# Batch 2's pair scatters, batch 3's in one expert slot, a declared wait, and a layer norm's two GpSimd steps: four small edits in an attention and expert kernel

## The chip, the cores and the metric

The kernel runs on one core of one Trainium2 chip. The metric is the device time of one execution in microseconds (us). A core has several engines that run side by side, each with its own queue of instructions in fixed order: TensorE (PE, matrix products), VectorE (DVE), ScalarE (ACT), GpSimd (POOL) and SyncE (SP, which here only issues DMAs). An instruction waits on semaphores for results of other engines.

## What is computed

The reference is one transformer block over x of 4 batches, 1024 positions and 256 channels, in float32:

```python
q_lat, k_lat, v_lat = ...                        # x @ W*_down: 16 heads with 64 latents each
q, k, v = ...                                    # 16 per head; half of q's and k's get a rotary embedding
scores = jnp.einsum('bhqd,bhkd->bhqk', q, k) * scale
scores = jnp.where(causal[None, None], scores, -jnp.inf)
y = jnp.einsum('bhqk,bhkd->bhqd', softmax(scores), v)
x = _layernorm(x + y @ Wc)
gates = _sinkhorn((x @ router_w.T + router_b) / temp)   # 3 iterations, over experts and over positions
topk_vals, topk_idx = jax.lax.top_k(gates, 2)
all_out = (relu(x @ wg[e]) * (x @ wp[e])) @ wo[e]       # 8 experts
x = _layernorm(x + sum over the two chosen experts of gate * all_out)
```

Only the two chosen experts count for a position, so the kernel computes only those.

## The kernel before

**Attention.** The batches are worked on one after the other, in units of a batch, a group of heads and a range of queries (`attend`, called from the main loop). The scores are computed twice: first for the maximum of each row (matmul L351, reductions L372 and L381 on DVE), then again, transposed, for the exponentials (matmul L456, ACT L467) and the products with the values (L436). While batch b is attended to, side work is fed in between by hand-written planners. A `Lane` is a list of generators; `give(budget)` lets it put instructions until the costs that the generators yield have used up the budget. `lane` carries projections and `finish`, `side` carries the routing, `places` the scatters. The order on each engine is then set by a scheduler that simulates a timeline from this program order, the priorities and the dependencies.

**The end of a batch's attention.** `finish` (L577 on) normalises the attention's output (L599 transposes, L604 and L606 on DVE), multiplies it with Wc (L615, L625), adds x (L628), and calls `layernorm` (L545 on): statistics on DVE (L549, L550), then two steps on POOL, the addition of epsilon to the variance (L552) and the power of minus one half (L553), then the scaling on DVE (L555). Its rows go to DRAM (`x_rows`, stores at L653 and L657).

**Routing and pairs.** `route` computes scores, Sinkhorn's iterations and the two best experts of each position, counts how many positions each expert has so far, and so gives each (position, choice) a row `ati` (tile `so_i`, L838) in a list in DRAM, `pairs`, that is ordered by expert. `scatter` (L842) writes an entry (the position's row, the row of the result, the gate) into that list: per batch 16 indirect DMAs of 128 entries each, issued on POOL (L848). After each it yields a cost: SCAT = 3.5 for batches 0 and 1, SCAT3 = 2.5 for batch 2, 1.0 for batch 3. For batches 0 to 2 `places.give(1.0)` comes at each step of the attention. Two marks order each scatter: `in_turn`, and `after(ins, latest[0])`, a dependency on the latest ACT instruction that the planner has put, so that it is not issued too early. `apart("pairs", ...)` (L561) declares that it has no dependency on any earlier scatter of pairs, since each touches rows of its own.

**The experts.** A `Slot` is 512 rows of one expert from the list: `first[0..7]` the first 512 of each (list 0, expert 0 to 7), `second[0..7]` the next 512 (list 1, expert 7 to 0), then further slots of 256 rows. `pairs_of` loads list entries (SP, L946), `gather` (L952) fetches the rows of x by indirect DMA on POOL (L957, four for 512 rows), `rows` transposes them (L1002) and splits them in a high and a low part, `slot` (L1005) computes: per quarter of the hidden width gate and linear products in three passes (`mm3`, L195 to L197), relu (ACT L1019), product (DVE L1020), split; then per 128 rows the output product, ACT's scaling by the gate (`eo`, L1038), and an indirect DMA that adds the rows to `results` in DRAM (POOL L1039). The adds of a slot wait for those of the slot before.

Batches 0 to 2 fill list 0 early enough for the first slots; batch 3 is attended to last, and its pairs come while the experts run: `slot` calls `places.give(1.0)` after each of its four quarters and each of its four blocks of 128 rows, in the slots `first[5]` and `first[6]`, so 16 times in all. What is left is put behind slot 6 (`places.until`). The load of list 1 for `second[0]` must wait for all of batch 3's pairs. A gather for a slot of list 0 beyond the third has a mark for the scheduler (not a semaphore) that it comes after `spread[0]`, the POOL step of the latest layer norm that is stored there: L552's addition.

Of the kernel before, what the change touches and what calls it, by code (L numbers as in the profile page):

```python
# [14 lines left out]
ALU = mybir.AluOpType  # L15
# [4 lines left out]
SIDE3 = 0.2  # L20
YB = 2
XG = 2
SCAT, SCAT3 = 3.5, 2.5
DZ = 3
HB = 6
SURE = 3
# [8 lines left out]
EPS_LN = 1e-5  # L35
# [6 lines left out]
def kernel(  # L42
# [16 lines left out]
    nc = tc.nc  # L59
    B, T, C = x_in.shape  # L60
# [3 lines left out]
    E, _, FF = wg_in.shape  # L64
# [38 lines left out]
    def mx_tile(name):  # L103
        return ps_mx.tile([P, QC], F32, tag="mx", name=name)
# [4 lines left out]
    def st_tile(name):  # L109
        return ps_st.tile([P, QC], F32, tag="st", name=name)  # L110
# [59 lines left out]
    neg_half = const.tile([P, BPQ], F32, name="neg_half")  # L170
# [15 lines left out]
    def split(hi, lo, src, sub=None):  # L186

        nc.scalar.copy(hi, src)  # L188
        (sub or nc.vector).tensor_tensor(lo, src, hi.bitcast(F32), ALU.subtract)  # L189

    def mm3(ps, terms):

        n = len(terms)
        for i, (sh, sl, mh, ml) in enumerate(terms):
            nc.tensor.matmul(ps, lhsT=sh, rhs=mh, start=(i == 0), stop=False)  # L195
            nc.tensor.matmul(ps, lhsT=sh, rhs=ml, start=False, stop=False)  # L196
            nc.tensor.matmul(ps, lhsT=sl, rhs=mh, start=False, stop=(i == n - 1))  # L197
# [210 lines left out]
    def in_turn(ins):  # L408

        if diagonal[0] is not None:  # L410
            tc.add_manual_dep(
                ins.ins, diagonal[0].ins.name,
                mybir.DependencyInfo(mybir.DependencyClass.NoSync, mybir.DependencyReason.SCHED_ONLY),
                reason="the attention goes first",
            )
# [127 lines left out]
    spread = [None]  # L543

    def layernorm(x, n):  # L545
        mv = small.tile([P, BPQ, 2], F32, tag="mv", name=f"mv_{n}", bufs=2)
        for i in range(BPQ):
            st = small.tile([P, 6], F32, tag="bnst", name=f"bnst_{n}_{i}")
            nc.vector.bn_stats(st, x[:, i, :])  # L549
            nc.vector.bn_aggr(mv[:, i, :], st)  # L550
        rstd = small.tile([P, BPQ], F32, tag="rstd", name=f"rstd_{n}", bufs=2)
        spread[0] = nc.gpsimd.tensor_scalar_add(rstd, mv[:, :, 1], EPS_LN)  # L552
        nc.gpsimd.tensor_tensor(rstd, rstd, neg_half, ALU.pow)  # L553
        for i in range(BPQ):
            nc.vector.tensor_scalar(  # L555
                x[:, i, :], x[:, i, :], mv[:, i, 0:1], rstd[:, i : i + 1], ALU.subtract, ALU.mult
            )
# [3 lines left out]
    def apart(what, kind, ins, others):  # L561

        seen = no_deps.setdefault(what, {})
        for o in others:
            for i in seen.get(o, ()):
                tc.declare_no_dep(ins.ins, i, reason="they touch rows of their own")
        seen.setdefault(kind, []).append(ins.ins)
# [9 lines left out]
    def finish(b, halves=range(NQC), alone=False):  # L577
# [3 lines left out]
        for half in halves:  # L581
# [58 lines left out]
            for i0 in range(0, BPQ, wide):  # L640
# [6 lines left out]
                for i in range(i0, i0 + wide):  # L647
                    f_out(i)
                    yield 0.9
            layernorm(x1, n)  # L650
            r0 = b * T + half * QC
            store = nc.sync if alone else nc.gpsimd
# [32 lines left out]
    def route(b):  # L685
# [152 lines left out]
        nc.vector.tensor_copy(ati, at)  # L838
        yield 0.0
        places.add(f"S{b}", scatter(b, ent, ati))  # L840

    def scatter(b, ent, ati):  # L842

        for n in range(NB):
            for k in range(2):
                while not hole[0]:
                    yield WAIT
                ins = nc.gpsimd.indirect_dma_start(  # L848
                    out=pairs[:, :],
                    out_offset=bass.IndirectOffsetOnAxis(ap=ati[:, k, n : n + 1], axis=0),  # L850
                    in_=ent[:, n, k, :], in_offset=None,
                )
                in_turn(ins)
                after(ins, latest[0])
                apart("pairs", "last" if b == B - 1 else "write", ins, ("last", "write", "early"))
                yield SCAT if b < B - 2 else SCAT3 if b < B - 1 else 1.0


    def tab(name, shape):
# [56 lines left out]
    def after(ins, other):  # L916
        tc.add_manual_dep(
            ins.ins, other.ins.name,
            mybir.DependencyInfo(mybir.DependencyClass.Sync, mybir.DependencyReason.DATA),
            reason="rows that both may touch",  # L920
        )
# [83 lines left out]
    def slot(k, between):  # L1005

        R = k.rows
        hs = []
        for f in range(NFC):
            cut = slice(f * P, (f + 1) * P)  # L1010
            if 2 * R > QC:
                gate, lin = (mx_tile(f"{i}p{k.name}_{f}") for i in "gl")
            else:
                both = mx_tile(f"gp{k.name}_{f}")
                gate, lin = both[:, :R], both[:, R:]
            for (h_, l_), ps in zip(k.hl, (gate, lin)):
                mm3(ps, [(h_[:, c, cut], l_[:, c, cut], k.xh[:, c, :R], k.xl[:, c, :R]) for c in range(CC)])
            r = early.tile([P, ER], F32, tag="relu", name=f"relu{k.name}_{f}", bufs=3)[:, :R]
            latest[0] = nc.scalar.activation(r, gate, AF.Relu)  # L1019
            nc.vector.tensor_tensor(r, r, lin, ALU.mult)  # L1020
            hh, hlo = (
                ffn.tile([P, ER], F32R, tag=i, name=f"{i}{k.name}_{f}", bufs=HB)[:, :R] for i in ("hh", "hl")
            )
            split(hh, hlo, r)
            hs.append((hh, hlo))
            next(between, None)
            if k in first[E - 3 : E - 1]:
                places.give(1.0)
        mine = []
        h_, l_ = k.hl[2]  # L1030
        for j in range(k.blocks):
            cut = slice(j * P, (j + 1) * P)
            if j % 2 == 0:
                both = st_tile(f"eo{k.name}_{j}")
            po = both[:, j % 2 * C : (j % 2 + 1) * C]
            mm3(po, [(hs[f][0][:, cut], hs[f][1][:, cut], h_[:, f], l_[:, f]) for f in range(NFC)])
            eo = early.tile([P, C], F32, tag="eo", name=f"eo{k.name}_{j}", bufs=EO)
            latest[0] = nc.scalar.activation(eo, po, AF.Copy, scale=k.ent[:, j, 2:3].bitcast(F32))  # L1038
            ins = nc.gpsimd.indirect_dma_start(  # L1039
                out=results[:, :], out_offset=bass.IndirectOffsetOnAxis(ap=k.ent[:, j, 1:2], axis=0),  # L1040
                in_=eo, in_offset=None, compute_op=ALU.add,
            )
            apart(f"results{k.name}", "add", ins, ("add",))
            if not k.which:
                apart("results", "early", ins, ("last",))
            for o in added:
                after(ins, o)
            mine.append(ins)
            next(between, None)
            if k in first[E - 3 : E - 1]:  # L1050
                places.give(1.0)
        added[:] = mine
        for _ in between:
            pass
# [59 lines left out]
    first = [Slot(0, e) for e in range(E)]  # L1114
# [13 lines left out]
    for i, unit in enumerate(units):  # L1128
        b, gs, qcs = unit
# [97 lines left out]
    def run(keys, given=()):  # L1227
        drain(begin(keys, 0, given))
        for n, key in enumerate(keys):
            slot(key, begin(keys, n + 1, given))  # L1230
            if key is first[E - 2]:
                places.until(f"S{B - 1}")
# [31 lines left out]
    for i in range(n_z):  # L1264
        z = zs.pop(i)
        mv = small.tile([P, BPQ, 2], F32, tag="mv", name=f"mv_f{i}", bufs=2)
# [4 lines left out]
        rstd = small.tile([P, BPQ], F32, tag="rstdz", name=f"rstd_f{i}", bufs=4)  # L1271
# [97 lines left out]
```

## Time and profile before

| | |
|---|---|
| time, median of 3 runs | 1090.79 us (1086.51 to 1091.84) |
| profiled execution | 1095.9 us, span 1094.2 us, 18114 instructions |
| mean granted TensorE clock | 0.957 |
| busy share PE, DVE, ACT, POOL | 89%, 67%, 57%, 44% |
| DMA moved | 119.67 MB, mean 109 GB/s |
| pairs on POOL (L848) | 64, 67.8 us in all, 1060 ns mean |
| adds to results on POOL (L1039) | 64, 107.2 us, 1674 ns mean |
| gathers on POOL (L957) | 64, 65.1 us, 1017 ns mean |
| POOL idle before pairs | 75.9 us, of which 57.5 us for ACT's L467 |

The profiled execution is one run; its own time is 5.1 us above the median of the timed runs. In a row of a timeline stand the start in us, the busy time, engine, line, operation, the tiles written and read, and in brackets the idle time of the engine before it and what ended it. "issue" there is time in which nothing that the profile shows was waited for, "remote" a release whose origin the profile does not see.

### The profile page before, as it was taken

How to read it: one execution, taken by the hardware profiler on the slowest of the kernel's cores; microseconds unless marked ns; L12 is line 12 of the kernel's file. 1: busy time of each engine (PE TensorE's matmuls, PEld its weight loads, DVE VectorE, ACT ScalarE, POOL GpSimd, SP SyncE). 2: the span in 40 equal slices, each digit the busy share in tenths (PEclk: the TensorE clock that was granted, in tenths of full speed). 3: DMA queues.
4: the chain of work that ended last, by engine and by line, in shares of the span. 5: the costliest groups of instructions: out<-in, count | busy, mean ns of one | idle time of the engine just before them, and what ended most of it. 6: DMA issues, size and time to landing. Idle time of an engine off the chain costs nothing.

```text
span 1094.2 us, 18114 instructions
## 1 busy us (share of the span) xinstructions
PE 975.8 (89%) x6436; PEld 608.2 (56%) x6436; DVE 734.9 (67%) x1622; ACT 625.4 (57%) x1314; POOL 479.1 (44%) x543
## 2 busy tenths in 40 slices
PE   6689999999999999989999996899999399999970
PEld 4555433455544455543444443488888288888860
DVE  4767787888888778787757882286686145555536
ACT  3445666765665755666656663656565145555533
POOL 6177511022352632552223215427557655554535
PEclk9889999999989999999999998999999699999985
DMA  6574420231240330333143220357555345656537
GB/s 245 165 213 121 117 86 18 76 117 33 95 121 17 107 114 5 127 80 98 47 102 98 46 70 2 99 174 186 141 125 123 69 109 113 172 113 164 123 36 307
DMA packets 71363, 119.67 MB, mean 109 GB/s; under 512 B 16416, under 2 KB 43040, under 8 KB 70880
## 3 DMA queue, kind: packets, MB, share of 16 engines
q1 hardware_dynamic: 48544, 81.76, 24.3%
q0 software_dynamic: 20672, 36.41, 15.5%
q8 instruction: 53, 0.87, 0.3%
q10 hardware_dynamic: 2048, 0.27, 0.2%
q14 instruction: 46, 0.38, 0.1%
HBM read 82.52 MB, written 35.60 MB: 108 GB/s over the span
## 4 chain that ended last, share of the span: by engine, by line
PE 74%; DMA 7%; DVE 6%; ACT 5%; SPq 4%; issue 2%; POOL 2%; another core or an unknown queue 1%; ACTq 0%; POOLq 0%; DVEq 0%
PE y L436 12%; PE s L351 11%; PE sT L456 10%; SPq L336 3%; PE gp L197 3%; PE gp L196 3%; PE gp L195 3%; PE eo L197 3%; PE eo L196 3%; PE eo L195 3%; PE po L625 3%; PE lp L197 2%; PE lp L196 2%; ACT pT L467 2%; PE lp L195 2%
## 5 line engine op out<-in xcount | busy, mean ns | idle before, releaser
L467 ACT ACTIVATE pT<-sT 128x512 f32<-128x512 f32 (+1 forms) x608 | 327.1, 575 | 180.8 <-PE sT L456 129.2
L372 DVE TENSOR_REDUCE mx<-s 128x1 f32<-128x384 f32 (+3 forms) x352 | 216.6, 633 | 36.2 <-PE s L368 35.1
L351 PE MATMUL s<-ks,qs 96*128 96x512 bf16 (+3 forms) x768 | 212.4, 333 | 19.4 <-DMA ks<-parts 10.8
L456 PE MATMUL sT<-qs,ks 98*128 98x512 bf16 (+3 forms) x768 | 215.5, 330 | 9.0 <-ACT pT L467 6.9
L381 DVE TENSOR_REDUCE mx<-s 128x1 f32<-128x512 f32 x256 | 171.4, 682 | 47.6 <-PE s L351 47.1
L474 POOL TENSOR_SCALAR_AFFINE_SELECT pT<-pT 128x512 f32<-128x512 f32 x112 | 70.7, 638 | 254.9 <-ACT pT L467 250.4
L436 PE MATMUL y<-pT,va 128*32 128x512 f32 (+3 forms) x1536 | 169.2, 503 | 4.4 <-ACT pT L467 3.1
L1039 POOL DMA_INDIRECT results<-eo,ents x64 | 107.2, 1674 | 82.6 <-ACT eo L1038 65.4
L351 PEld LDWEIGHTS <-qs 96*128 96x128 bf16 x768 | 70.8, 99 | 120.3 <-issue 89.7
L456 PEld LDWEIGHTS <-ks 98*128 98x128 bf16 x768 | 69.8, 99 | 89.6 <-issue 57.4
L848 POOL DMA_INDIRECT pairs<-ent,so_i x64 | 67.8, 1060 | 75.9 <-ACT pT L467 57.5
L368 PE MATMUL s<-mask,ident_b 128*128 128x128 bf16 (+2 forms) x352 | 87.1, 248 | 0.0
L1020 DVE TENSOR_TENSOR relu<-relu,lp 128x512 f32<-128x512 f32 x64 | 43.7, 683 | 60.1 <-ACT relu L1019 30.6
L195 PE MATMUL eo<-wh,hh 128*128 128x256 f32 x280 | 80.5, 289 | 0.9 <-ACT eo L1038 0.6
L957 POOL DMA_INDIRECT xg<-x_rows,ents x64 | 65.1, 1017 | 33.6 <-issue 16.1
L196 PE MATMUL eo<-wl,hh 128*128 128x256 f32 x280 | 79.0, 284 | 0.0
L189 DVE TENSOR_TENSOR wl<-w,wh 128x512 fp32r<-128x512 f32 x108 | 69.3, 684 | 14.3 <-ACT wh L188 13.8
L197 PE MATMUL eo<-wh,hl 128*128 128x256 f32 x280 | 77.7, 284 | 0.0
L1019 ACT ACTIVATE relu<-gp 128x512 f32<-128x512 f32 (+1 forms) x76 | 42.7, 563 | 59.6 <-PE gp L197 49.9
L436 PEld LDWEIGHTS y<-pT,va 128*32 128x32 f32 x1536 | 31.8, 108 | 64.6 <-issue 46.5
L195 PE MATMUL gp<-xh,wh 128*128 128x512 f32 (+1 forms) x176 | 65.0, 376 | 2.1 <-ACT xh L188 1.2
L196 PE MATMUL gp<-xl,wh 128*128 128x512 f32 (+1 forms) x176 | 65.6, 374 | 0.0
(213 smaller groups left out, 1849.0 us busy)
## 6 DMA issues: line engine op xcount, KB each, us to landing
ks<-parts SPq DMA_DIRECT2D x90, 128.0 KB
w<-in_wg_dram SPq DMA_DIRECT2D x18, 512.0 KB
w<-in_wp_dram SPq DMA_DIRECT2D x18, 512.0 KB
w<-in_wo_dram SPq DMA_DIRECT2D x18, 512.0 KB
qs<-parts SPq DMA_DIRECT2D x66, 128.0 KB
parts<-lv POOLq DMA_DIRECT2D x12, 384.0 KB
parts<-lv POOLq DMA_DIRECT2D x24, 192.0 KB
xh<-in_x_t_dram SPq DMA_DIRECT2D x8, 512.0 KB
```

What stands on the lines that cost most here:

```text
L195: nc.tensor.matmul(ps, lhsT=sh, rhs=mh, start=(i == 0), stop=False)
L196: nc.tensor.matmul(ps, lhsT=sh, rhs=ml, start=False, stop=False)
L197: nc.tensor.matmul(ps, lhsT=sl, rhs=mh, start=False, stop=(i == n - 1))
L351: nc.tensor.matmul(ps, lhsT=q(h, half)[:NROW, t * P : (t + 1) * P], rhs=k(h, kc)[:NROW, :w], start=first, stop=last,)
L368: nc.tensor.matmul(each[:, :, w - P :], lhsT=ident_b, rhs=mask.unsqueeze(1).to_broadcast([P, m, P]), start=False, stop=True,)
L372: nc.vector.tensor_reduce(mx_of[:, half, h0 : h0 + m, t], each, AX.X, ALU.max)
L381: nc.vector.tensor_reduce(mx_of[:, kc, h, t : t + 1], ps, AX.X, ALU.max)
L436: nc.tensor.matmul(acc[g, qc][SLOT * h : SLOT * (h + 1), lo:], lhsT=va[b % 2][:, kb, at : at + SLOT], rhs=pT[:, h, lo:], start=(kb == 0), ...
L456: nc.tensor.matmul(st[:, h % m * w : (h % m + 1) * w], lhsT=k(h, kb // BPQ)[: NROW + 2, kb % BPQ * P : (kb % BPQ + 1) * P], rhs=q(h, qc)[: ...
L467: latest[0] = nc.scalar.activation(pT[:, h + 1 - m : h + 1, lo:], st[:, : m * w].rearrange("p (h t) -> p h t", t=w), AF.Exp, scale=scale,)
L474: diagonal[0] = nc.gpsimd.affine_select(out=block, in_=block, pattern=[[0, HG], [1, P]], compare_op=ALU.is_ge, fill=0.0, base=0, channel_m ...
L1039: ins = nc.gpsimd.indirect_dma_start(out=results[:, :], out_offset=bass.IndirectOffsetOnAxis(ap=k.ent[:, j, 1:2], axis=0), in_=eo, in_offs ...
```

## The change

Four edits. The cost of a pair of batch 2 becomes 2.0 instead of 2.5, so `places.give` puts them at a closer distance in the attention's steps. Each scatter declares a wait for the landing of the last but one of the same batch (`after(ins, sent[-2])`), ahead of the call of `apart`. A pair of batch 3 costs 0.5 instead of 1.0, and only slot 6 gives, so that each of its eight calls puts two pairs. And `spread[0]` names the layer norm's second POOL step (the power) instead of its first, so that gathers for the later slots come behind both.

```diff
-SCAT, SCAT3 = 3.5, 2.5
+SCAT, SCAT3 = 3.5, 2.0
...
         rstd = small.tile([P, BPQ], F32, tag="rstd", name=f"rstd_{n}", bufs=2)
-        spread[0] = nc.gpsimd.tensor_scalar_add(rstd, mv[:, :, 1], EPS_LN)
-        nc.gpsimd.tensor_tensor(rstd, rstd, neg_half, ALU.pow)
+        nc.gpsimd.tensor_scalar_add(rstd, mv[:, :, 1], EPS_LN)
+        spread[0] = nc.gpsimd.tensor_tensor(rstd, rstd, neg_half, ALU.pow)
...
     def scatter(b, ent, ati):
 
+
+        sent = []
         for n in range(NB):
             for k in range(2):
...
                 in_turn(ins)
                 after(ins, latest[0])
+                if len(sent) > 1:
+                    after(ins, sent[-2])
+                sent.append(ins)
                 apart("pairs", "last" if b == B - 1 else "write", ins, ("last", "write", "early"))
-                yield SCAT if b < B - 2 else SCAT3 if b < B - 1 else 1.0
+                yield SCAT if b < B - 2 else SCAT3 if b < B - 1 else 0.5
...
             next(between, None)
-            if k in first[E - 3 : E - 1]:
+            if k is first[E - 2]:
                 places.give(1.0)
...
             next(between, None)
-            if k in first[E - 3 : E - 1]:
+            if k is first[E - 2]:
                 places.give(1.0)
```

## The prediction

> **What bounds the kernel now.** I read the page's busy shares first (PE 975.8 us of a span of 1094.2), then the table of windows of 10 us, PE's list of waits between 640 and 900 us, and last the timelines of the engines around the places that the change touches. In the table the columns are: window, its length, PE, PEld, DVE, ACT, POOL busy with counts, PEclk, DMA share, GB/s.
>
> ```profile
> 650.00:660.00 10.00, 9.80 (x91) 5.39 (x90) 5.18 (x26) 6.61 (x15) 5.69 (x7) 1.00 0.02 3
> 660.00:670.00 10.00, 4.13 (x36) 2.06 (x33) 1.20 (x5) 1.20 (x2) 7.57 (x9) 0.83 0.03 2
> 670.00:680.00 10.00, 8.06 (x42) 4.57 (x42) 3.89 (x12) 4.96 (x10) 3.04 (x4) 0.66 0.02 2
> ...
> 840.00:850.00 10.00, 10.00 (x58) 8.78 (x57) 4.45 (x7) 3.18 (x6) 8.17 (x7) 1.00 0.71 180
> 850.00:860.00 10.00, 4.41 (x26) 3.72 (x25) 3.29 (x5) 4.14 (x8) 8.17 (x7) 0.89 0.43 69
> 860.00:870.00 10.00, 0.00 (x0) 0.00 (x0) 0.00 (x0) 0.00 (x0) 4.43 (x5) 0.50 0.35 50
> 870.00:880.00 10.00, 6.94 (x27) 4.93 (x28) 1.29 (x2) 1.55 (x3) 7.56 (x9) 0.59 0.35 106
> ```
>
> PE is full nearly everywhere, so work and order on PE set the time, but for two holes, both beside POOL's indirect DMAs: 660 to 675, where batch 2's pairs are scattered, and 854 to 871, after batch 3's. PE's waits name them.
>
> ```profile
> PE xgT_ps L1002 <- DMA xg<-x_rows,ents: 18.7, 5, 16.4
> PE yt_ps L599 <- DVE yn L606: 5.6, 1, 5.6
> PE y L436 <- ACT pT L467: 3.1, 1, 3.1
> ```
>
> The 16.4 us is the second hole, the 5.6 the first, and the 3.1 a smaller third one at 702.6, beside gathers. The changed program, built and laid beside the old one, has PE, DVE, ACT and SP in unchanged order up to the experts' stage; POOL's order first differs in batch 2's pairs. So four places are to be costed.
>
> **The new wait.** It adds nothing: `apart`, called right behind, declares no dependency between this scatter and every earlier one of its kind, the last but one among them. With the lines of `sent` deleted the built program is the same, instruction for instruction. Even a working wait would find its pair landed: the pair of 655.23 has landed by 657.3, and the next but one starts at 657.82. Behind it on POOL would stand the later pairs, the layer norm's steps, for which DVE L555 waits, and the gathers, for which PE's xgT waits. Cost 0.
>
> **Batch 2's pairs (2.5 to 2.0).** Each pair waits for an ACT instruction that the planner put ahead of it. Before, the waits let twelve go back to back, 1.27 us each, and the thirteenth waits until ACT moves again. First POOL, then DVE and ACT:
>
> ```profile
> 669.20 0.96 POOL L848 DMA_INDIRECT pairs<-ent,so_i  x1 [0.30 <-issue]
> 673.45 0.96 POOL L848 DMA_INDIRECT pairs<-ent,so_i  x1 [3.29 <-ACT pT L467]
> ```
>
> ```profile
> 669.62 0.26 DVE L604 RECIPROCAL rec<-yt_ps 128x16 f32<-128x16 f32 x1 [8.70 <-remote]
> ```
>
> ```profile
> 672.57 1.09 ACT L467 ACTIVATE pT<-sT 128x512 f32<-128x512 f32 x2 [8.77 <-PE yt_ps L599]
> ```
>
> PE had ended the matmuls for which ACT and DVE wait by 664.9, and was itself idle for 5.62 us from there. They start 5 to 8 us later, when the burst stops. The same is seen at 699.86 (ACT 5.2 us idle behind gathers) and at 886.41 (relu 3.8 us late). In the mixed run of pairs and adds from 831 to 862 there is no such delay. I read it so: some 6 us into an unbroken run of indirect DMAs, PE's releases no longer reach the others until the run stops. The mechanism is not shown; the rows are. Here a rule of the Trainium skill speaks against me: "SBUF — State Buffer", section "Who interferes with whom", says that DMA never contends with a compute engine, and PE and ACT wait for nobody; at most descriptor generation on POOL suffers. By the rule a longer burst costs PE nothing and this edit is worth 0; by the row the freeze lasts as long as the burst. I take the row.
>
> In the changed program the first seven pairs wait for no ACT instruction, the eighth to fourteenth for instructions that all ended before the freeze (the same counts let the twelfth go at 669.20), the fifteenth for none; only the sixteenth waits for a later one. Fifteen in a row: 3 x 1.27 = 3.8 us longer, and the hole on PE grows by it. Bounds: -2 if the freeze ends by itself, since DVE's release at 669.62 lies before the twelfth's end, and the last pairs no longer break up 673 to 682; +4.5 with the slower clock behind it (0.66 at 670 to 680). I take **+3.8**.
>
> Then the sixteenth goes about 677, before 681.33, the list's load and the gathers begin sooner, and the two stores of rows (L653, L657) stand behind seven gathers instead of four, so that runs of seven and five replace four and eight. The third hole (3.14 us) may shrink by 1 to 3, or move: I take **-1**, from -3 to +1.
>
> **Layer norm.** The two POOL steps with the gathers between them:
>
> ```profile
> 729.26 0.24 POOL L552 TENSOR_SCALAR rstd<-mv 128x4 f32<-128x4 f32 x1 [25.80 <-DVE mv L550]
> ...
> 735.33 1.06 POOL L553 TENSOR_TENSOR rstd<-rstd,neg_half 128x4 f32<-128x4 f32 x1
> ```
>
> Now L553 follows at once: 735.33 - 729.5 = 5.8 us sooner, and the four gathers (1.27 us each) come 1.06 later. DVE L555, the router and Sinkhorn's small steps start up to 5.8 us earlier. PE is full from 707 to 854, though, and what comes out, batch 3's positions (so_i, ready at 816.9), waits: in the changed order the pairs stand behind the experts' relu of slot 6 (826.3 + 0.6). So it gives nothing. What it can take: a Sinkhorn transpose, put some 10 us earlier in PE's order, could meet a DVE that isn't ready. **0**, from 0 to +2; without the cover of the full PE it would have been -5.8.
>
> **Batch 3's pairs in slot 6 alone.** This is the tail of POOL's run, from its timeline, and then, from the chain that ended last (start, us, what), the two transfers behind it:
>
> ```profile
> 850.51 1.60 POOL L1039 DMA_INDIRECT results<-eo,ents  x1 [0.30 <-issue]
> ...
> 860.48 1.58 POOL L1039 DMA_INDIRECT results<-eo,ents  x1 [0.30 <-issue]
> 862.36 0.98 POOL L848 DMA_INDIRECT pairs<-ent,so_i  x1 [0.30 <-issue]
> 868.00 0.99 POOL L957 DMA_INDIRECT xg<-x_rows,ents  x1 [4.66 <-DMA ents<-pairs]
> ```
>
> ```profile
> 862.36 2.16 DMA pairs<-ent,so_i
> 864.53 2.60 DMA ents<-pairs
> ```
>
> PE's work ends at 854.4; from there the end is POOL's: the last pair, its landing, the load of list 1, gathers, and PE at 870.84. POOL has no pause from 831 on, and slot 6's first add starts at 850.51, 5 us after its eo (ACT 845.06 + 0.48). The change puts pairs 1 to 8 behind slot 4's and 5's adds, and the other eight two by two behind each add of slot 6. An add is 1.58 + 0.30 = 1.88, a pair 0.97 + 0.30 = 1.27. The add eo_5_0 waits for the landing of eo_4_3 (3.04 us idle at 831.24); moved ahead of the pairs it goes at about 825.1. Then come 8 pairs and 4 adds, 10.2 + 7.5 = 17.7: POOL is at slot 6's first add by 843 to 845, and now waits for ACT until 845.8. Ahead of the last pair stand 4 adds and 7 pairs: 845.8 + 7.5 + 8.9 = 862.2; the second add waits 0.5 more (ACT 850.28 + 0.48), and two or three pairs take 1.43 to 1.49 as now (+0.7). That is 863.4, **+1.1** on 862.36; bounds -0.2 (no stretching) and +2.5. PE's slots 5 to 7 and the work on each side of the hole are unchanged.
>
> The second half from 886 on has a full PE; a weight load and two adds trade places: 0, within 1.
>
> **Sum**: 3.8 - 1 + 0 + 0 + 1.1 = +3.9 us. The profiled execution took 1095.9 (span 1094.2 and 1.7 around it); it becomes 1099.8. It lies 5.1 above the median of 1090.8; the difference carried over, 1094.7.
>
> **Rivals.**
> *The burst costs nothing in an unprofiled run* (or its freeze does not grow). For it: no mechanism is shown. Against: the profiled run is only 5.1 us above the median, and the late releases cost PE 12.8 us by its idle times (5.62 + 1.35 + 0.73 from 664.9 to 673, 3.14 + 0.55 around 700, 1.43 at 886), so most of it is there without the profiler. Then only the tail counts: about 1091.9.
> *Slower: POOL comes late to slot 6.* At 818.58 and 820.73 two pairs took 1.84 and 3.04 us instead of 0.97. If the eight pairs after eo_5_0 stretch alike (0.9 to 2.1 each), POOL passes 845.8; from there, so from about 2 us of stretching on, each microsecond lands in the hole. Four such pairs bring some 4 us more: 1098.7. For: DVE's splits run beside them. Against: the pairs from 833 to 862 took at most 1.49.
> *Faster: the early finish of batch 2's pairs counts.* If the freeze ends by itself, the third hole goes (-3.7) and the last four pairs' pauses with it (-2), against the tail's +1.1: 1086; were the burst's freeze to go altogether (-7.7), 1079. For: DVE's release at 669.62. Against: ACT's at 672.57.
>
> **Numbers.** Forecast 0.46 (1094.7, own range 1091 to 1098.5), no growth 0.20, slower 0.18, faster 0.16. What this measurement can tell from no change is about 0.5%, 5.5 us: faster is below 1085.3, slower above 1096.2. Faster takes 0.14 from its case; slower all of its own, most of it above, plus a third of the forecast: 0.33; the rest, 0.53, is same. Range 1085 to 1101.
>
> **What would show it.** Fifteen pairs without a pause from about 655, DVE L604 idle 11 to 13 us and PE's 5.6 grown to 9 or so; L553 right behind L552; the last pair 8.5 to 10 us after PE's last matmul of slot 7 and PE's 16.4 at 17 to 18. Wrong, if the hole at 660 has the same size with fifteen pairs, or if pairs are seen spaced by landings.

## The result, and the profile after

The changed kernel takes 1095.24 us (median of 18 runs, 1089.64 to 1099.44), the kernel before 1089.36 in 18 runs beside it. The ratio is 1.0051, with a 95% interval from 1.0035 to 1.0067: 5.6 us slower, 3.8 to 7.3. The forecast was +3.9 us.

PE's waits between 640 and 900 us, as before: the hole before list 1 has grown from 16.4 to 18.4, and the wait at the pairs has come apart into three, of 3.51, 2.05 and 5.17 us: 10.7 together, where it had been 5.62, 1.35 and 0.73, or 7.7.

```profile
PE xgT_ps L1007 <- DMA xg<-x_rows,ents: 20.1, 4, 18.4
PE sT L456 <- ACT pT L467: 7.9, 3, 5.2
PE yt_ps L599 <- DVE rec L604: 3.5, 1, 3.5
PE ynT_ps L615 <- DVE x L628: 2.1, 1, 2.1
```

In the windows of 10 us, PE's busy time (the first number behind the length) falls to 2.34 from 660 to 670, where it was 4.13, and ACT does nothing at all there. The first pair went 3.4 us earlier in this profile than in the one before (651.82 against 655.23), so the same window does not hold quite the same work.

```profile
660.00:670.00 10.00, 2.34 (x14) 1.22 (x15) 1.71 (x5) 0.00 (x0) 7.57 (x9) 0.66 0.03 2
670.00:680.00 10.00, 6.82 (x37) 3.50 (x37) 2.75 (x8) 4.79 (x10) 1.49 (x2) 0.66 0.08 9
...
870.00:880.00 10.00, 4.53 (x13) 2.66 (x14) 1.29 (x2) 1.07 (x2) 7.45 (x8) 0.50 0.29 86
```

POOL's timeline at the end of batch 2's pairs, and ACT's and DVE's beside it. Fifteen pairs run from 651.82 without a pause; the row at 669.57 is the fifteenth. ACT stands still for 12.91 us where it had been 8.77. DVE, though, starts again at 663.22, while the pairs still run: it was idle for 5.76 us where it had been 8.70.

```profile
669.57 0.96 POOL L850 DMA_INDIRECT pairs<-ent,so_i  x1 [0.30 <-issue]
674.01 0.96 POOL L850 DMA_INDIRECT pairs<-ent,so_i  x1 [3.48 <-ACT ynT L618]
```

```profile
672.43 1.31 ACT L467 ACTIVATE pT<-sT 128x512 f32<-128x512 f32 x2 [12.91 <-remote]
```

```profile
663.22 0.26 DVE L604 RECIPROCAL rec<-yt_ps 128x16 f32<-128x16 f32 x1 [5.76 <-remote]
```

Layer norm and tail, again from POOL's timeline. The power step now follows the addition at once (730.41). Slot 6's first add, third row, starts at 847.92 after a pause of 3.00 us, and the last pair at 864.76.

```profile
730.09 0.24 POOL L552 TENSOR_SCALAR rstd<-mv 128x4 f32<-128x4 f32 x1 [25.30 <-DVE mv L550]
730.41 1.05 POOL L553 TENSOR_TENSOR rstd<-rstd,neg_half 128x4 f32<-128x4 f32 x1
...
847.92 1.62 POOL L1044 DMA_INDIRECT results<-eo,ents  x1 [3.00 <-issue]
...
864.76 0.96 POOL L850 DMA_INDIRECT pairs<-ent,so_i  x1 [0.30 <-issue]
870.41 0.98 POOL L962 DMA_INDIRECT xg<-x_rows,ents  x1 [4.69 <-DMA ents<-pairs]
```

One profiled execution against one other says little about 5 us: the first pair of batch 2 stands at 655.23 in one and at 651.82 in the other, and up to there the programs are the same. So I cut each profile at three rows of POOL that every kernel has: the first pair of batch 2, the addition L552 of the last layer norm, and the first gather of list 1. The stage of the pairs is from the first to the second, the stage of the experts from the second to the third.

| kernel (chip) | pairs' stage, us | experts' stage, us |
|---|---|---|
| before (A) | 74.0 | 138.7 |
| after (A) | 78.3 | 140.3 |
| e1, batch 2's pairs alone (B) | 79.0 | 138.3 |
| e2, batch 3 in slot 6 alone (B) | 75.2 | 141.7 |
| e3, layer norm alone (B) | 75.1 | 138.2 |
| e4, a rest after each pair (B) | 80.0 | 142.8 |
| e5, rest after four (C) | 64.4 | 137.3 |
| e6, and between gathers (C) | 66.5 | 136.6 |
| e7, batch 3's pairs in slot 5 (C) | 65.4 | 127.0 |
| e8, e6 and e7 (C) | 65.9 | 126.8 |
| e9, after again (D) | 79.0 | 140.1 |
| e10, as e5 (D) | 72.4 | 138.2 |
| e11, the wait made real (D) | 75.4 | 139.9 |
| e12, as e8 (D) | 65.1 | 126.2 |

The letters stand for the first runs (A) and for three groups of four kernels (B, C, D), each on a chip of its own; whether A is one of these chips is not known. Each row is one profile, and the cut is by place in the program and not by work: where matmuls move across it, as in e4, part of one stage's growth belongs to the other. The kernel before had medians of 1087.7 on B, 1078.3 on C and 1090.2 on D.

### The profile page after: what moved, and what is told of

Its sections match the earlier page's. It is cut to its first block, busy times and chain, and to the rows that moved or that the text cites. A ratio compares the mean times of both kernels' runs of the same rounds, so it can differ in the third digit from the quotient of the medians.

```text
span 1093.4 us, 18106 instructions
## 1 busy us (share of the span) xinstructions
PE 974.7 (89%) x6436; PEld 607.4 (56%) x6436; DVE 734.0 (67%) x1622; ACT 625.7 (57%) x1314; POOL 472.4 (43%) x543
## 4 chain that ended last, share of the span: by engine, by line
PE 75%; DMA 6%; ACT 5%; DVE 5%; issue 3%; SPq 2%; POOL 2%; another core or an unknown queue 1%; ACTq 0%; POOLq 0%; DVEq 0%
PE y L436 13%; PE s L351 11%; PE sT L456 11%; PE gp L196 3%; PE gp L197 3%; PE gp L195 3%; PE eo L195 3%; PE eo L196 3%; PE eo L197 3%; PE po L625 3%; PE lp L197 2%; PE lp L196 2%; ACT pT L467 2%; PE lp L195 2%; PE s L368 2%
## 5 line engine op out<-in xcount | busy, mean ns | idle before, releaser
L351 PE MATMUL s<-ks,qs 96*128 96x512 bf16 (+3 forms) x768 | 212.3, 333 | 17.3 <-DMA ks<-parts 8.5
L850 POOL DMA_INDIRECT pairs<-ent,so_i x64 | 63.3, 989 | 70.0 <-ACT pT L467 46.9
L189 DVE TENSOR_TENSOR hl<-relu,hh 128x512 fp32r<-128x512 f32 (+1 forms) x76 | 48.5, 646 | 28.0 <-ACT hh L188 23.2
L188 ACT CAST wh<-w 128x512 fp32r<-128x512 f32 x108 | 60.6, 619 | 7.3 <-PE gp L196 3.9
```

Source lines behind the costliest of these rows:

```text
L351: nc.tensor.matmul(ps, lhsT=q(h, half)[:NROW, t * P : (t + 1) * P], rhs=k(h, kc)[:NROW, :w], start=first, stop=last,)
```

## The experiments

**e1 to e3: each part alone.** My theory: an unbroken run of indirect DMAs freezes PE's releases for as long as it lasts, so the pairs carry most of the loss; rivals: the tail carries it, or the freeze is the profiler's. The edits (e2's condition stands at two places):

```diff
e1: -SCAT, SCAT3 = 3.5, 2.5
    +SCAT, SCAT3 = 3.5, 2.0
e2: -yield ... else 1.0
    +yield ... else 0.5
    -if k in first[E - 3 : E - 1]:
    +if k is first[E - 2]:
e3: -spread[0] = nc.gpsimd.tensor_scalar_add(...)
    -nc.gpsimd.tensor_tensor(rstd, rstd, neg_half, ALU.pow)
    +nc.gpsimd.tensor_scalar_add(...)
    +spread[0] = nc.gpsimd.tensor_tensor(rstd, rstd, neg_half, ALU.pow)
```

> The kernel before with batch 2's pairs at cost 2.0 alone. If the freeze lasts as long as the unbroken run of pairs: fifteen pairs in a row, ACT idle 12 to 13 us (8.8 before), PE's late start some 3.8 us later, and the time 3 to 4.5 us above the kernel before. If the run's length doesn't matter, or the freeze is the profiler's own: within 1 us of it.

> The kernel before with batch 3's pairs two by two in slot 6 alone. If slot 6's first add stands behind the landing of slot 5's last one: PE's hole before list 1 of 18 to 18.5 us (16.4 before), time 1.5 to 2.5 us up. If it waits only for ACT, as forecast: hole of 17.5, 1.1 us up. In both cases the run of batch 2's pairs stays at twelve.

> The kernel before with the layer norm's two POOL steps together and nothing else. If a full PE hides it: within 1 us of the kernel before, though the power step comes 5 us sooner. If the earlier router work counts: 3 to 5 us less. If transposes put too early stall PE: 1 to 2 us more, as idle PE between 735 and 755.

Measured against the kernel before: e1 1.0045 (1.0024 to 1.0066), some 4.9 us; e2 1.0025 (1.0014 to 1.0036), 2.7 us; e3 0.9996 (0.9984 to 1.0009), nothing. Together 7.2, and the whole change 5.6 and 7.2 (e9): they add up within their intervals. e1's 4.9 lies a little above the 3 to 4.5 expected, with its interval of 2.6 to 7.2 around them. In e1 ACT is idle 13.59 us beside fifteen pairs:

```profile
668.07 1.08 ACT L467 ACTIVATE pT<-sT 128x512 f32<-128x512 f32 x2 [13.59 <-remote]
```

One regularity holds in the six profiles on A, B and D with this train (before, e2 and e3 with twelve pairs, after, e1 and e9 with fifteen). ACT starts again 17.1 to 17.3 us after the first pair with twelve, and 20.6 to 21.4 us after it with fifteen, each time 1.9 to 2.6 us behind the end of the last pair of the train. DVE's L604 starts again 11.4 to 14.4 us after the first pair, whether twelve or fifteen follow. So it is ACT's wait that grows with the train; DVE's does not.

In e2 PE's hole is 19.3 us, longer than either case expected, and the run of batch 2's pairs stays at twelve. POOL is through with the pairs ahead of slot 6's first add at 843.6, its eo is ready at 843.0 (ACT 842.56 + 0.47), and it starts at 845.87, so it did not wait for ACT's eo alone. The view names a relu of ACT as what ended the wait; in the changed kernel the same add starts ahead of that relu (847.92 against 848.01), so the relu is not what it waits for:

```profile
845.87 1.61 POOL L1039 DMA_INDIRECT results<-eo,ents  x1 [2.24 <-ACT relu L1019]
```

In e3 the power step comes right behind the addition, PE is busy 10.00 of 10.00 us in every window from 715 to 755, and the experts' stage is unchanged: a full PE hides the earlier layer norm, as forecast.

**e4: a rest after each pair.** The kernel before, with a real dependency of each pair of batch 2 on the landing of the one ahead of it. To be real it must be left out of `apart`, which now skips what is in `keep`:

```diff
+keep = sent[-1:] if b == B - 2 else []
+for o in keep:
+    after(ins, o)
-apart("pairs", ..., ins, ("last", "write", "early"))
+apart("pairs", ..., ins, ("last", "write", "early"), keep)
```

> The kernel before, but each pair of batch 2 truly waits for the landing of the one ahead of it, which puts 1.2 us or so of rest between two. If an unbroken run of indirect DMAs holds up PE's releases: no ACT or DVE idle over 3 us there, PE's 5.6, 1.35 and 0.73 gone, and the time 5 to 8 us below the kernel before. If the number of pairs counts and not the rest between them: the freeze lasts as long or longer, the pairs end some 10 us later, and the time is 0 to 5 us above. If the freeze is the profiler's: the profile shows it gone, the time within 1 us.

Measured: 1.0065 (1.0044 to 1.0087), 7 us slower, which none of the three expectations gave. The profile shows what went and what came. POOL's rows show the rests, and ACT waits 3.4 us at most from 646 to 697: the freeze is gone. But the sixteenth pair leaves at 691.51, 45.3 us after the first (26.1 before), and PE then stands before the first expert's rows. Its experts' stage is longer too, by 4.4; PE has no wait over 0.5 us in it ahead of the tail's hole, but its pairs' stage holds 390 matmul records where the kernel before has 418, so part of that is work that moved across the cut.

```profile
650.99 0.96 POOL L851 DMA_INDIRECT pairs<-ent,so_i  x1 [1.40 <-DMA pairs<-ent,so_i]
653.35 0.96 POOL L851 DMA_INDIRECT pairs<-ent,so_i  x1 [1.41 <-DMA pairs<-ent,so_i]
...
691.51 0.96 POOL L851 DMA_INDIRECT pairs<-ent,so_i  x1 [1.90 <-ACT pT L467]
697.41 1.25 POOL L964 DMA_INDIRECT xg<-x_rows,ents  x1 [4.94 <-DMA ents<-pairs]
```

```profile
702.97 1.18 PE L1009 MATMUL xgT_ps<-ident,xg 128*128 128x128 f32 x4 [6.78 <-DMA xg<-x_rows,ents]
```

The row at 653.35 also gives the landing: 1.41 + 0.96 = 2.37 us from a pair's start to the next one's release.

**e5 to e8: rests that cost less, and the tail.** e5 puts the pairs early and has a group of four wait for the last of the group before; e6 does the same between the gathers of two slots (`gone` holds the last gather of the slot before); e7 puts all sixteen pairs of batch 3 into slot 5, since slots 5 and 6 still give and each call now puts two; e8 is e6 and e7.

```diff
e5: -SCAT, SCAT3 = 3.5, 2.5
    +SCAT, SCAT3 = 3.5, 0.5
    +keep = sent[len(sent) // 4 * 4 - 1 :][:1] if b == B - 2 and len(sent) >= 4 else []
e6: +for o in gone[-1:]:
    +    after(ins, o)
e7: -yield ... else 1.0
    +yield ... else 0.5
```

> The kernel before with batch 2's pairs put early (cost 0.5) and a true wait for landing after every fourth, so that runs of four (5 us) alternate with rests of about 1.1 us, and the pairs still end by 680. If an unbroken run of 6 us or more holds up PE's releases: no idle over 3 us on ACT or DVE during the pairs, and 5 to 9 us below the kernel before. If rests are of no use and the first gathers simply follow the pairs: within 2 us.

> As e5, and the gathers of a slot wait for the last gather's landing of the slot before it, so that their runs of eight and twelve become fours. If the unbroken run is the cause there too: another 2 to 4 us below e5. If the later gathers cost more than the freeze: 1 to 3 us above e5.

> The kernel before with two pairs of batch 3 for each call in slot 5, so that all sixteen stand ahead of slot 6's adds on POOL. If POOL's queue sets the hole before list 1: the last pair leaves near 848 by the times of before (16 x 1.27 + 5 x 1.88 from 818.6) and not at 862, the hole of 16.4 falls to 2 to 5 us, and the time by 10 to 13 us. If the gather is bound by something else (buffer, list load): the hole stays over 12.

> e6 and e7 together. If freeze and tail are separate stretches, the gains add up: 16 to 25 us below the kernel before. If the tail's hole takes up what the freeze gives (a later start of batch 3's pairs), no more than e7 alone.

Measured: e5 0.9978 (0.9962 to 0.9994), e6 the same; e7 0.9922 (0.9892 to 0.9952); e8 0.9897 (0.9866 to 0.9928). e5 gave 2 us where I had expected 5 to 9, e6 nothing more where I had expected 2 to 4, and e8 11 us where I had expected 16 to 25; e7's profile says why. Its program is that of before, on every engine, until the experts' slots. Yet on this chip POOL and the windows read:

```profile
664.66 0.96 POOL L848 DMA_INDIRECT pairs<-ent,so_i  x1 [0.30 <-issue]
665.65 0.27 POOL L552 TENSOR_SCALAR rstd<-mv 128x4 f32<-128x4 f32 x1
```

```profile
650.00:660.00 10.00, 9.88 (x77) 6.37 (x76) 4.46 (x13) 6.45 (x15) 7.56 (x9) 1.00 0.03 2
660.00:670.00 10.00, 7.55 (x64) 3.14 (x63) 2.41 (x7) 5.80 (x12) 6.81 (x8) 0.96 0.10 10
```

The row at 664.66 is the fifteenth pair, again without a pause since 646.94, since ACT's instructions were done in time. And PE (9.88) and ACT (6.45) work beside them; ACT has no wait of 2 us from 640 to 712. There is no freeze in this profile of chip C. The pairs' stage is 65.4 us long there, against 74.0 to 75.2 on A and B: 9 to 10 us, as much as the kernel before is faster on C (1078.3 against 1087.7). A run without rests is thus needed for the freeze (in e4, with rests, it went) but does not suffice; the chips of B and D have it, and that of C has not. So e5 had no freeze to remove. e7's tail is as expected in kind: PE's longest wait before list 1 is 6.6 us instead of 16.4, and the experts' stage is 10.3 us shorter than in e5 on the same chip; the time fell by 8, short of the 10 to 13 expected. The last pair left 32.6 us after the first (801.28), later than the sum of 29.7, since two pairs took 1.83 and 3.04 us, as before:

```profile
833.90 0.96 POOL L848 DMA_INDIRECT pairs<-ent,so_i  x1 [0.30 <-issue]
```

**e9 to e12: the same on another chip.**

> The changed kernel again, on whatever chip comes. If the freeze belongs to some chips only: with it (the kernel before near 1088), ACT idle 12 to 13 us in the pairs and 4 to 7 us above the kernel before; without it (before near 1078), fifteen or more pairs in a row with ACT and PE at work beside them, and only the tail's 2 to 3 us above it. If the freeze follows from the program alone: 12 to 13 us idle again, whatever the level of before.

> The kernel of e5 again. On a chip with the freeze (before near 1088): ACT's 8.8 us idle gone and 6 to 10 us below the kernel before, if rests of 1.1 us after four pairs are enough. On a chip without it: 0 to 3 us below, as in e5. If the rests do nothing for a freeze: ACT idle over 5 us in the pairs again.

> The changed kernel with its wait made real: the last but one is left out of the list of those declared independent, nothing else changed. If a pair lands 2.0 to 2.3 us after its start and the next but one would start after 2.53 anyway: pairs still at 1.27 us, freeze and time as in the changed kernel of the same call, within 2 us. If the wait holds pairs up: they come at 1.4 us or more, the freeze shortens or goes where there is one, and the time falls by 4 us or more.

> The kernel of e8 again. On a chip without the freeze: 9 to 10 us below the kernel before, as in e8. On one with it: the tail's 8 to 10 and the freeze's 6 to 10 together, 14 to 20 us below. If the two are not separate: no more than 10 either way.

Chip D has the freeze. e9, the changed kernel, takes 1.0066 (1.0041 to 1.0090), and ACT is idle 13.56 us:

```profile
673.94 1.08 ACT L467 ACTIVATE pT<-sT 128x512 f32<-128x512 f32 x2 [13.56 <-remote]
```

e10 takes 0.9954 (0.9939 to 0.9969), 5 us less, a little under what I had expected. With runs of four the freeze beside the pairs is gone, and then the twelve gathers in a row from 680.62 bring one of their own:

```profile
697.34 0.60 ACT L467 ACTIVATE pT<-sT 128x512 f32<-128x512 f32 x1 [5.12 <-remote]
```

e12 has rests there too and shows none: no ACT wait over 2.4 us from 640 to 712. This is its first rest, 1.1 us more than the usual 0.30:

```profile
656.40 0.96 POOL L851 DMA_INDIRECT pairs<-ent,so_i  x1 [1.40 <-DMA pairs<-ent,so_i]
```

It takes 0.9838 (0.9812 to 0.9863), 18 us less, and its pairs' stage, 65.1 us, is that of chip C. e8 and e12 are one kernel: worth 11 us (8 to 14) where there is no freeze and 18 (15 to 20) where there is. These are timed runs and no profiles. The kernel before is 11.9 us faster on C than on D (1078.3 against 1090.2), and with rests the two chips are only 3.7 us apart (1068.6 against 1072.2): that leaves little room for a freeze that is only the profiler's. This kernel has the lowest median on both chips, on C only just (1068.6 against 1070.2 for e7).

e11 is the changed kernel with its wait made real (`sent[-2:-1]` as keep, in all four batches). The time, 1.0096 (1.0066 to 1.0127; six runs from 1093.4 to 1105.5), is not below e9's. The first seven pairs go at 1.27 us as expected; the eighth to fourteenth come after 1.26 to 1.91 us, since some wait for a landing or for ACT, and the fifteenth after 5.76:

```profile
663.96 0.96 POOL L852 DMA_INDIRECT pairs<-ent,so_i  x1 [0.95 <-DMA pairs<-ent,so_i]
```

In that profile, which is of the fastest of the six runs, the freeze comes in pieces of 4 to 6 us and the stage is 75.4 us, not 79.0. The times don't show this; with this spread the question whether the real wait helps is undecided. That it makes the kernel 4 us faster is not supported.

**Is it a load of code?** An engine that waits for its next instructions would stand still too. In the six profiles named above no packet of the instruction queues that the profile shows (q8, q14) moves between the train's first pair and ACT's new start; the next one comes 2 to 7 us after that start (in the kernel before at 678.8, ACT at 672.57). So ACT was not released by the arrival of instructions. Beside the train the pairs' own packets are the only ones, at 3.4% of the DMA engines' time or less in any 2 us, so DMA bandwidth was not short either.

**The tail, seen closer.** Why did slot 6's first add start at 847.92 when its eo was ready at 846.0? Each add of a slot waits for the landings of the adds of the slot before. Slot 5's last add was issued at 840.31. The DMA view of the kernel after, from 842.3 to 844, shows 332 GB/s, of which POOL's queue (q0) has next to nothing:

```profile
DMA packets 321, 0.57 MB, mean 332 GB/s; under 512 B 46, under 2 KB 46, under 8 KB 321
...
q0 software_dynamic: 30, 0.00, 1.3%
```

From 844 to 846.5 the 0.14 MB on that queue follow, and then no queue moves anything until 847.9:

```profile
q0 software_dynamic: 208, 0.14, 37.4%
```

So most of the add's 128 KB moved when SP's weight loads had ended, and the next slot's add went 7.6 us after its issue (7.7 in e9, 6.4 in e2), some 1.4 us after the last packet. That the weight loads held it back is read from this order and not tested. In the kernel before, slot 6's first add came 4.9 us after slot 5's last with no pause on POOL.

## Why the prediction was right, and where its sum was off

*The wait, 0.* The declared wait isn't in the program; e11 shows that the real one isn't a gain in time either. My remark that a working wait would always find its pair landed was too strong: from the eighth pair on it sometimes did not.

*Batch 2's pairs, +3.8.* Right in size, and in mechanism for ACT only. Fifteen unbroken pairs came, and PE's idle time beside them grew from 7.4 us (mean of before, e2 and e3, which have the same program there) to 11.2 (mean of after, e1 and e9): +3.8. But PE's releases did not all wait until the run stopped. DVE got its release in mid-train, so that the sign I had named, L604 idle for 11 to 13 us, did not come (5.8 in after, 7.9 in e1, 7.8 in e9), and PE's 5.6 did not grow to 9: a second idle time of 4.5 to 5.2 us came behind it, for ACT's pT. The rule of the Trainium skill ("SBUF — State Buffer", section "Who interferes with whom") speaks of contention for SBUF's ports. That no burst can hold PE up was my own inference from it, and the runs on A, B and D contradict that inference; whether a port has any part in it no run here shows. The freeze was taken for a property of the program; it is one of program and chip. That the changed kernel was measured on chips that have it is luck: on one like C, where the program before already ran fifteen pairs in a row and no freeze showed (e7), this term would have had nothing to grow; the changed kernel was not run there.

*The gathers, -1.* Right: PE's idle time at the third hole fell from 3.4 us (mean of before, e2 and e3; 3.69 in before, with the 0.55 ahead of it) to 2.4 (after, e1 and e9). But the pairs' stage grew by 3.9 (74.8 to 78.7) and not by 2.8. The rest is PE's busy time for the same matmuls, 1.2 us more in the means (62.8 to 63.9), at a mean granted clock of 0.87 in the stage where it had been 0.89 to 0.93. By chip it is uneven, 2.5 on A and 0.4 on B. The sum had put the slower clock behind a longer hole at nothing and named it only in the upper bound of +4.5; that the clock is the whole reason is not shown.

*Layer norm, 0.* Right: 0.9996.

*The tail, +1.1.* Right in direction, too small. The experts' stage grew by 1.8 (after and e9 against 138.4, the mean of before, e1 and e3), and by 3.3 in e2. The term that was mis-sized is the start of slot 6's first add: "now waits for ACT until 845.8". In after its eo was ready at 846.0, and it waited till 847.92, by all signs for the landing of slot 5's last add. The four adds and seven pairs behind it took 16.84 us, where I had 16.4 and 1.2 of stretching and waits.

By stages: 3.9 + 1.8 = 5.7 us, and the timed runs gave 5.6 and 7.2. The sum was thus too small by PE's longer busy time, which goes with the lower clock (1.2), and by the tail (0.7). That the forecast of 1094.7 us lies only 0.5 below the median is in part luck, since the kernel before came out 1.4 us faster beside it than the 1090.8 on which I had built. The rival *no growth of the freeze* fell with e1, *faster by an early finish* too: the sixteenth pair did go early (22.2 us after the first, not 26.1) and it didn't count. The slower rival, stretched pairs that make POOL late to slot 6, was not the cause: POOL was at slot 6's first add by 844.9 and had to wait.

## What to carry to other kernels

When one engine issues a long train of indirect DMAs, look at the others' idle times beside it and not only at its own queue: here rests of about 1.1 us after every fourth, between the pairs and between the gathers, went with a stage 10 us shorter (65.1 in e12 on D, against 74.0 to 75.2 on A and B for the program before), while a rest after each made the last pair 19 us later and left PE waiting 6.8 us for its data. What an accumulate must wait for is the landing of the one before, so count with the landing under the load of that moment and not with the issue. Compare profiles from more than one chip before taking a stall for the program's. A wait that is declared next to a statement of independence for the same pair may not be in the program at all: read the built program before costing it.

## What the runs showed of the hardware

Beside 12 to 15 unbroken indirect DMAs of 1.27 us each, ACT and DVE started 5 to 13 us after the PE matmuls they waited for, in A, B and D: DVE while the train still ran, ACT 1.9 to 2.6 us after its end. On the chip of C the same program had PE at 9.88 of 10 us beside the same train. With rests of about 1.1 us, after each pair in B or after every four in D, there was none beside the pairs. Why one chip differs, and what in the chip holds the releases, stays open; no run here tells it. A landing of a 128 KB accumulate took between about 4.6 us (eo_5_0 behind eo_4_3, before) and 7.6 us under weight loads (slot 5's last add, after), from issue to the next one's release.
